# Layer 0's edge stage in a four-layer graph kernel: another order of the turn, lists in finer steps, and list work moved between two stages

## The chip, the cores and the metric

The kernel runs on one core of a Trainium2 chip. The metric is device time in microseconds (us), the median of three runs; lower is better. The core has a matrix engine (PE, with PEld for its weight loads), a vector engine (DVE), an activation engine (ACT), a general engine (POOL, here mostly for gathers by index) and a queue for transfers (SP). They run side by side and wait for one another through semaphores.

## The reference

Four graph layers follow one another on N = 4096 nodes with C = 256 channels and an adjacency matrix `adj` of N x N. Each is followed by a residual sum and a layer norm. The change concerns layer 0, which has 8 heads of 32 channels and 6 curvature features a node:

```python
h = (x @ W.T).reshape(n, H, D)
e_l = jnp.einsum('nhd,hd->nh', h, a_l)
e_r = jnp.einsum('nhd,hd->nh', h, a_r)
logits = jax.nn.leaky_relu(e_l[:, None, :] + e_r[None, :, :], negative_slope=0.2)
curv_pair = jnp.abs(curv_feats[:, None, :] - curv_feats[None, :, :])
logits = logits + gate * jnp.einsum('ijf,hf->ijh', curv_pair, Wc)
logits = jnp.where((adj > 0)[:, :, None], logits, jnp.float32(-1000000000.0))
attn = jax.nn.softmax(logits, axis=1)
out = jnp.einsum('ijh,jhd->ihd', attn, h).reshape(n, H * D)
...
x = _layernorm(x + out, axis=-1)
```

The adjacency is sparse, about 0.4% on average, and its first rows and columns are much denser than the rest: an edge (i, j) has the probability 0.0039 w_i w_j, where w falls as the inverse root of the node's number and has mean 1.

## The kernel before

**Stages of layer 0.** A prologue projects x and writes a table of node rows (264 values with the factor of the softmax, 8 head scores, 6 features) to memory. Then `rows0` works out the first chunk of 128 rows densely, in 32 tiles of columns, on times 187 to 436 us of the profile. After it `rows_by_edges`, the edge stage, works out the other 31 chunks by their edges, from about 440 to 1690 us. Meanwhile two background lanes prepare what comes later:

- Lane one, `list_edges`, makes the edge list of each chunk. `Lists.edges` turns adjacency rows into bf16; `Lists.steps` (L935) finds the columns of each row's edges (`max_index`, L943, 424 of them in all), sorts them (L949 to 960), counts them and writes `what` (node numbers by rank, and running starts), `half` and `from_middle`. Two small products on PE belong to it: `flags` (L923), 32 of one column each, which tell which tiles hold edges, and `last` (L973), running sums of the edge counts. After each fourth chunk `places` (L983) numbers the nodes that hold edges in pairs of chunks.
- Lane two, `list_pairs`, makes for the later layers, by `list_pair` (L1011), a list of the nodes that each pair of chunks needs: `rhs` (L1018 to 1022), four `here` (L1034), 32 products on PE (L1028) and a few steps on DVE. Each entry becomes a job `listed_mask`: a gather `pair_m` on POOL (L1055), and six jobs later a convert `pair_mb` on DVE (L1059) and a write by SP (L1060).

`lane` gives both lanes a step now and then. Its rates are steps per call: (3.0, 0.7) in `rows0`, one call a tile, and (1.4, 0.3) in the edge stage, one call for each tile of edges. Each call also does a pair job and a dense-mask job. `ends` (end steps of finished chunks, with layer 1's projection of them) takes a step a call as well.

**A turn of the edge stage.** A chunk's edges are cut into tiles of 128; blocks have 5 to 10 tiles, 64 blocks with 445 tiles in all. A block goes through these steps, in this logical order:

- `middle` (L615): ACT writes u, the distance of an edge number from the middle of each row's edges.
- `spread` (L621): DVE compares u with `half` (`of_row`, 1 where an edge belongs to a row, L624), and PE multiplies it by `what` (x, L627, two matmuls a tile), which gives each edge its row's list and values.
- `nodes` (L629): ACT copies the row's values (side, L632); DVE picks from x the column node of each edge (k L634, hit L636 and L638, node L640, idx L642).
- `gather` (L644): POOL issues one indirect gather a tile from the table into g, of which there are three buffers.
- `differences` (L650): DVE d (L654), PE transposes it (d_p, L656), ACT takes the positive part (dT, L658). `pair_terms` (L660): PE two products (e_p), ACT exponential (e, L666).
- `weights` (L668): DVE w, two steps. `values` (L675): DVE scales g by w (L678).
- `rows` (L680): ACT builds to_row, one activation a tile (L685) and one relu (L686). `add` (L688): PE sums g by row, two matmuls a tile (L691).

**What sets the order.** For PE, DVE and ACT the program order is written out (`manual_schedule`): what stands in the code first runs first on each of them. POOL and SP take their work in an order that the framework chooses. In turn i (L712 to 746) the code does spread(i+3), lane, differences(i+1), values(i), gather(i+2), pair_terms(i+1), lane, nodes(i+3), lane, add(i), rows(i+1), weights(i+1), middle(i+4), lane; the first three lane parts have n // 4 calls each, the last has the rest.

Of the kernel before, what the change touches and what calls it, by code (L numbers as in the profile page):

```python
# [49 lines left out]
F32 = mybir.dt.float32  # L50
# [6 lines left out]
ALU = mybir.AluOpType  # L57
AX = mybir.AxisListType
PSUM = bass.MemoryType.PSUM
DRAM = bass.MemoryType.DRAM  # L60

P = 128
IC = 512
# [15 lines left out]
def gnn_stack(ctx: ExitStack, tc: tile.TileContext, a: dict, out: bass.AP):  # L79
    nc = tc.nc  # L80
# [512 lines left out]
    def rows_by_edges(prepared, pair_w, neg_bound, ends, ps, lane):  # L593
# [8 lines left out]
        with ExitStack() as st:  # L602
# [8 lines left out]
            class Block:  # L611
# [3 lines left out]
                def middle(self):  # L615
# [2 lines left out]
                    self.u = two.tile([P, BT, P], F32, name="u", bufs=1)  # L618
                    nc.scalar.activation(self.u[:, 0:self.n], number[:, 0:self.n], AF.Abs, bias=self.lists.from_middle[:, self.b:self.b + 1])

                def spread(self):  # L621
                    n, ls = self.n, self.lists
                    of_row = two.tile([P, BT, P], F32, name="of_row")
                    nc.vector.tensor_scalar(of_row[:, 0:n], self.u[:, 0:n], ls.half, None, ALU.is_lt)  # L624
                    self.x = ps_x.tile([P, n, ls.K + SIDE], F32, name="x")
                    for t in range(n):
                        nc.tensor.matmul(self.x[:, t], of_row[:, t], ls.what, start=True, stop=True)  # L627

                def nodes(self):  # L629
                    n, K = self.n, self.lists.K  # L630
# [76 lines left out]
            def at(i, *what):  # L707
                if 0 <= i < B:
                    for w in what:
                        getattr(plan[i], w)()  # L710

            with tc.manual_schedule(engines={mybir.EngineType.PE, mybir.EngineType.DVE, mybir.EngineType.Activation}):  # L712
                for i in range(3):
                    at(i, "middle", "spread", "nodes")
                    if i < 2:
                        at(i, "gather")
                at(3, "middle")
                at(0, "differences", "pair_terms", "rows", "weights")
                late = []
                for i, blk in enumerate(plan):  # L720
                    c, n = blk.c, blk.n
                    share = n // 4
                    ends.put.extend(late)
                    late = []
                    at(i + 3, "spread")
                    lane(share)
                    at(i + 1, "differences")
                    blk.values()
                    at(i + 2, "gather")
                    at(i + 1, "pair_terms")  # L730
                    lane(share)
                    at(i + 3, "nodes")
                    lane(share)
                    if blk.t0 == 0:
                        ends.until(c - 2)
                        accs[c] = ps_acc.tile([P, VW], F32, name="acc")
                    last = blk.t0 + n == EDGE_TILES[c]
                    blk.add(accs[c], last)
                    if last:
                        acc = accs.pop(c)  # L740
                        late.append((lambda acc=acc: acc.rearrange("p (h d) -> p h d", h=H0), c))
                    at(i + 1, "rows", "weights")
                    at(i + 4, "middle")
                    lane(n - 3 * share)
                ends.put.extend(late)
                ends.until(NC)
                drain(ends.steps)

    def layer0(proj):
        lin = 1.0 - 0.2  # L750
        with ExitStack() as st:
# [119 lines left out]
            lists = st.enter_context(tc.tile_pool(name="l0_list", bufs=2))  # L871
            pool = st.enter_context(tc.tile_pool(name="l0_ps", bufs=1, space=PSUM))
            ps = tags(pool, ["pa", "pb"])
            lists_ps = st.enter_context(tc.tile_pool(name="l0_list_ps", bufs=1, space=PSUM))

            jobs, dense_jobs = [], []

# [6 lines left out]
            class Lists:  # L884
# [37 lines left out]

                def flags(self):  # L923

                    pf = ps([P, NT], "flags")
                    for T in range(NT):
                        nc.tensor.matmul(pf[:, T:T + 1], self.columns(T), ones_b[:, 0:1], start=True, stop=True)
                    return pf
# [6 lines left out]
                def steps(self, f):  # L935
                    c, K, kind = self.c, self.K, EDGE_PARTS[self.c]
                    S = sum(kind)
                    near = self.near
                    cand = lists.tile([P, S, 8], U16, name="cand")
                    cost = 0  # L940
                    for s, (at, W) in enumerate(self.spots):

                        nc.vector.max_index(cand[:, s], ones8, near[:, at:at + W])  # L943
                        cost += W + 100
                        if cost > 900:
                            cost = 0
                            yield
                    val = lists.tile([P, S, 8], F32, name="val", bufs=1)
                    nc.vector.tensor_tensor(val, widths[kind].unsqueeze(2).to_broadcast([P, S, 8]), cand, ALU.is_gt)  # L949
                    node = lists.tile([P, S, 8], F32, name="val_n", bufs=1)  # L950
                    nc.vector.tensor_tensor(node, firsts[kind].unsqueeze(2).to_broadcast([P, S, 8]), cand, ALU.subtract)
                    flags = self.flags()
                    nc.vector.tensor_mul(val, val, node)

                    top = lists.tile([P, KMAX], F32, name="top")
                    flat = val.rearrange("p s e -> p (s e)")
                    for k in range(0, K, 8):
                        nc.vector.max(top[:, k:k + 8], flat)
                        if k + 8 < K:
                            nc.vector.match_replace(flat, top[:, k:k + 8], flat, 0.0)  # L960
                            if k == 8:

                                nc.vector.tensor_scalar(f[:, c % BL, :], flags, 0.0, None, ALU.is_gt)
                                nc.vector.tensor_reduce(there[:, c:c + 1], flags, AX.X, ALU.add)
                            if k > 0:
                                yield
                    n_c = listed[:, c:c + 1]
                    hit = lists.tile([P, KMAX], F32, name="top_on")
                    nc.vector.tensor_scalar(hit[:, 0:K], top[:, 0:K], 0.0, None, ALU.is_gt, ALU.add, accum_out=n_c)
                    n_b = lists.tile([P, 1], BF16, name="n_b")  # L970
                    nc.vector.tensor_copy(n_b, n_c)
                    last = ps([P, 1], "last")
                    nc.tensor.matmul(last, upto, n_b, start=True, stop=True)  # L973
                    nc.vector.tensor_scalar(self.what[:, 0:K], top[:, 0:K], -1.0, float(N), ALU.mult, ALU.add)
                    nc.vector.tensor_scalar_mul(self.half, n_c, 0.5)
                    nc.vector.tensor_sub(self.what[:, K:K + 1], last, n_c)
                    mid = lists.tile([P, 1], F32, name="mid")
                    nc.vector.scalar_tensor_tensor(mid, last, -1.0, self.half, ALU.mult, ALU.add)
                    for b, (t0, _) in enumerate(blocks_of(c)):
                        nc.vector.tensor_scalar_add(self.from_middle[:, b:b + 1], mid, t0 * P + 0.5)  # L980
                    yield

            def places(k, f):  # L983
# [5 lines left out]
                yield  # L989
                W = BP * NT  # L990
                flat = g.rearrange("p b t -> p (b t)")
                upto_p = ps([P, W], "upto_p")
                nc.tensor.matmul(upto_p, upto, flat, start=True, stop=True)
                total_p = ps([P, W], "total_p")
                nc.tensor.matmul(total_p, ones_b, flat, start=True, stop=True)
                x = lists.tile([P, W], F32, name="place")
                nc.vector.tensor_tensor_scan(x, go_on.rearrange("p b t -> p (b t)"), total_p, 0.0, ALU.mult, ALU.add)
                nc.vector.tensor_copy(sizes[:, k * BP:(k + 1) * BP], x.rearrange("p (b t) -> p b t", t=NT)[:, :, NT - 1])
# [12 lines left out]
            def list_pair(q):  # L1011
# [9 lines left out]
                nc.vector.tensor_tensor(rhs[:, :, 0, :], rhs[:, :, 1, :], tiles.unsqueeze(2).to_broadcast([P, NT, A]), ALU.mult)  # L1021
                nc.vector.tensor_scalar_mul(rhs[:, :, 1, :], rhs[:, :, 1, :], row)
                yield
                pl = lists_ps.tile([P, 2, A], F32, name="list_p")

                def products(k, here):
                    for T in range(k * Q, (k + 1) * Q):
# [3 lines left out]
                for k in range(4):  # L1031
                    T = slice(k * Q, (k + 1) * Q)
                    here = lists.tile([P, Q, P], BF16, name="here", bufs=4)
                    nc.vector.tensor_tensor(here, count.unsqueeze(1).to_broadcast([P, Q, P]),  # L1034
                                            at[:, 1, b, T].unsqueeze(2).to_broadcast([P, Q, P]), ALU.is_equal)
                    due.append((k, here))
                    yield
                    if len(due) > 1:
                        products(*due.pop(0))
                products(*due.pop(0))  # L1040
                yield
                x = lists.tile([P, 2, A], F32, name="list")
                nc.vector.tensor_copy(x, pl)
# [132 lines left out]
                    ls.whole = True  # L1176
                return ls

            rows0(FIRST, ends, ps, lambda n: lane(n, (3.0, 0.7)), 2)

            def lane_e(n):
                for _ in range(n):
                    lane(1, (1.4, 0.3))
                    ends.step()

            rows_by_edges(prepared, pair_w, neg_bound, ends, ps, lane_e)
# [503 lines left out]
```

## Time and profile before

| what | value |
|---|---|
| runs | 3717.66, 3719.96, 3713.12 us; median 3717.66 |
| the profiled execution's own time | 4065.58 us |
| its span, first to last instruction | 4063.8 us |
| mean granted clock of PE | 0.78 |
| `rows0` | 187 to 436 us |
| edge stage, first to last `values` | 463.3 to 1673.8 us |
| gathers of g (L647) | 445, 482.2 us on POOL, 1084 ns each |
| pair gathers (L1055) | 251, 282.9 us on POOL, 1127 ns each |
| finds (L943) | 424, 192.9 us on DVE, 471 ns each |

The profiled execution is 348 us longer than the median, so a stage's length in it is not its length in a timed run. In the views, L12 is line 12 of the kernel; `out<-in` are the program's names; a wait reads "engine, what waited <- what released it: total us, times, longest". Lines of the timeline read "start, length, engine, line, operation, out<-in shapes, how many", with the idle time before and its releaser in square brackets. "issue" is time in which an engine waited for nothing that the profile shows; "remote" names a release that it doesn't trace to an instruction.

### The profile page before, as it was taken

Reading aid. Unit: us, or ns where it says so; the run is one execution under the profiler, and the core shown is the slowest. Engines: PE = TensorE matmul, PEld = TensorE weight load, DVE = VectorE, ACT = ScalarE, POOL = GpSimd, SP = SyncE. Lnnn points to the kernel's source line nnn. Section 1 sums busy time; section 2 is a strip of 40 time slices with the busy share of each in tenths; the row PEclk is TensorE's granted clock in tenths of the full one; section 3 lists DMA queues with packets and bytes.
Section 4 is the critical chain, followed back from the end, with each engine's and each line's share of the span. In section 5 each row is a group of like instructions: output and inputs, shape, how many; then the busy total and the mean of one; then the engine's idle time right before and its main releaser. Section 6 shows DMA issues by size and latency. Waiting matters only on the chain. (4 is left out here: it accounts for less than half of the span.)

```text
span 4063.8 us, 53164 instructions
## 1 busy us (share of the span) xinstructions
PE 2855.1 (70%) x15878; PEld 2107.2 (52%) x15878; DVE 2372.0 (58%) x7423; ACT 1320.8 (33%) x3748; POOL 1928.4 (47%) x1874
## 2 busy tenths in 40 slices
PE   7566544454666757677768887877688978987886
PEld 5355433343454545466653333333467757775664
DVE  5277677676555544345447888787444544544555
ACT  3344333343333334334443222223312231222233
POOL 0000465544676766234425755543166626643663
PEclk7577655666676666688878888989799989988998
DMA  4344577554334333244433333332334434434443
GB/s 140 94 139 138 162 236 235 178 151 148 106 107 111 108 107 97 85 148 125 123 95 114 99 97 97 94 91 70 116 106 115 110 116 113 120 83 138 137 140 90
DMA packets 348334, 495.62 MB, mean 122 GB/s; under 512 B 120828, under 2 KB 256866, under 8 KB 348034
## 3 DMA queue, kind: packets, MB, share of 16 engines
q0 software_dynamic: 87600, 252.16, 22.2%
q1 hardware_dynamic: 242008, 223.19, 18.7%
q10 hardware_dynamic: 18432, 16.79, 1.2%
q8 instruction: 131, 2.15, 0.2%
q14 instruction: 163, 1.34, 0.1%
HBM read 426.20 MB, written 65.72 MB: 121 GB/s over the span
## 5 line engine op out<-in xcount | busy, mean ns | idle before, releaser
L1271 POOL DMA_INDIRECT g<-table,pair_idx x1010 | 1106.7, 1096 | 814.2 <-issue 162.8
L647 POOL DMA_INDIRECT g<-table,idx x445 | 482.2, 1084 | 346.1 <-PE acc L691 183.1
L1560 PE MATMUL acc<-g,w 128*128 128x257 f32 x2448 | 599.7, 394 | 53.7 <-DVE w L1554 28.5
L1560 PEld LDWEIGHTS acc<-g,w 128*128 128x128 f32 x2448 | 470.3, 196 | 145.7 <-DVE w L1554 41.2
L1055 POOL DMA_INDIRECT pair_m<-in_adjT,cell x251 | 282.9, 1127 | 527.2 <-DVE mb L386 269.5
L1461 DVE SCALAR_TENSOR_TENSOR w<-R,g,mask 128x256 f32<-128x256 f32 x1004 | 425.1, 494 | 26.7 <-PE den L1474 19.5
L1554 DVE SCALAR_TENSOR_TENSOR w<-R,g,mask 128x256 f32<-128x256 f32 x612 | 281.4, 481 | 194.8 <-PE acc L1560 132.3
L1470 PE MATMUL num<-w,g 128*64 128x256 f32 x2008 | 326.5, 431 | 58.8 <-DVE w L1461 40.4
L203 PE MATMUL ph<-wx,xT 128*128 128x258 f32 (+3 forms) x640 | 255.8, 538 | 151.6 <-ACT xT L199 113.7
L691 PE MATMUL acc<-g,to_row 128*128 128x264 f32 x890 | 345.5, 567 | 10.6 <-issue 5.6
L1560 PE MATMUL acc<-V,w 128*128 128x257 f32 x1152 | 296.4, 398 | 32.8 <-DMA R<-r_d 11.5
L691 PEld LDWEIGHTS acc<-g,to_row 128*128 128x128 f32 x890 | 253.8, 294 | 81.5 <-issue 8.5
L627 PE MATMUL x<-what,of_row 128*128 128x40 f32 (+4 forms) x890 | 165.4, 361 | 165.8 <-DVE of_row L624 86.5
L1470 PEld LDWEIGHTS num<-w,g 128*64 128x64 f32 x2008 | 160.5, 151 | 207.6 <-DVE w L1461 110.3
L627 PEld LDWEIGHTS x<-what,of_row 128*128 128x128 f32 x890 | 158.1, 273 | 205.8 <-DVE of_row L624 92.7
L1560 PEld LDWEIGHTS acc<-V,w 128*128 128x128 f32 x1152 | 226.2, 200 | 74.4 <-ACT V L1540 18.1
L203 PEld LDWEIGHTS ph<-wx,xT 128*128 128x128 f32 x640 | 150.8, 257 | 214.3 <-ACT xT L199 145.1
L1570 ACT ACTIVATE y<-acc,inverse 128x256 f32<-128x256 f32 x96 | 45.5, 474 | 543.3 <-PE acc L1560 204.7
L1554 DVE SCALAR_TENSOR_TENSOR w<-R,V,mask 128x256 f32<-128x256 f32 x288 | 136.0, 480 | 121.3 <-PE acc L1560 56.5
L658 ACT ACTIVATE dT<-d_p 36x128 f32<-36x128 f32 (+5 forms) x64 | 17.2, 269 | 562.7 <-PE d_p L656 326.6
L943 DVE FIND_INDEX8 cand<-ones,near 128x8 uint16<-128x520 bf16 (+8 forms) x424 | 192.9, 471 | 0.0
L199 ACT ACTIVATE xT<-xT_p 128x128 f32<-128x128 f32 x384 | 102.7, 274 | 202.0 <-remote 107.1
(324 smaller groups left out, 4732.2 us busy)
## 6 DMA issues: line engine op xcount, KB each, us to landing
ai<-in_adj SPq DMA_DIRECT2D x124, 512.0 KB
mask<-listed_d SPq DMA_DIRECT2D x228, 128.0 KB
at<-in_adjT SPq DMA_DIRECT2D x96, 256.0 KB
mask<-mask_d SPq DMA_DIRECT2D x128, 128.0 KB
g<-table,pair_idx POOLq DMA_INDIRECT x1010
R<-r_d SPq DMA_DIRECT2D x56, 256.0 KB
table<-V POOLq DMA_DIRECT2D x12, 1032.0 KB
s<-y ACTq DMA_DIRECT2D x96, 128.0 KB
```

Of the source, the lines that this page charges most:

```text
L199: nc.scalar.activation(xT[:, kt, :], pt[:, kt, :], AF.Copy, accum_out=self.xs[:, kt, T:T + 1])
L203: nc.tensor.matmul(ph, xT[:, kt, :], self.wx[:, kt, :], start=kt == 0, stop=kt == 1 and self.bias is None)
L627: nc.tensor.matmul(self.x[:, t], of_row[:, t], ls.what, start=True, stop=True)
L647: nc.gpsimd.indirect_dma_start(self.g[:, t, :], None, table0[:, :], bass.IndirectOffsetOnAxis(ap=self.idx[:, t:t + 1], axis=0))
L691: nc.tensor.matmul(acc, self.to_row[:, t], self.g[:, t, 0:VW], start=self.t0 + t == 0, stop=last and t == n - 1)
L943: nc.vector.max_index(cand[:, s], ones8, near[:, at:at + W])
L1055: nc.gpsimd.indirect_dma_start(m[:, :], None, pair_cells, bass.IndirectOffsetOnAxis(ap=cell[:, k:k + 1], axis=0))
L1271: nc.gpsimd.indirect_dma_start(g[:, :], None, self.table[:, :], bass.IndirectOffsetOnAxis(ap=pair_idx[:, at:at + 1], axis=0))
L1461: nc.vector.scalar_tensor_tensor(w[:, h], R[:, h].rearrange("p t i -> p (t i)"), g[:, VW2 + h:VW2 + h + 1], m, ALU.max, ALU.mult)
L1470: nc.tensor.matmul(num[h % 2 * D2:(h % 2 + 1) * D2, h // 2, :], g[:, h * (D2 + 1):h * (D2 + 1) + D2], w[:, h], start=False, stop=last and ...
L1554: nc.vector.scalar_tensor_tensor(w, R[:, q * PW:(q + 1) * PW], g[:, C + 1:C + 2], m, ALU.max, ALU.mult)
L1560: nc.tensor.matmul(t, w[:, it * P:(it + 1) * P], g[:, 0:C + 1], start=k == 0, stop=last)
```

## The change

Four things change.

1. The order of the turn. `choose` (the of_row comparison) is taken out of `spread` and done one turn ahead. Turn i now does spread(i+3), values(i), add(i), lane, differences(i+1), choose(i+4), middle(i+5), lane, pair_terms(i+1), rows(i+1), nodes(i+3), gather(i+3), lane, weights(i+1), lane. So the gather is three blocks ahead in place of two (g keeps its three buffers), `middle` five ahead in place of four, `rows` comes ahead of `nodes`, and `add` comes right after `values`.
2. Lists in finer steps. The flags products are issued at the start of a list. There is a yield, an end of a lane step, between DVE's operands and the product that reads them (`last`), and between products and their readers (`last`, `places`). The 32 list products come in one go after the last `here` and a yield, instead of eight a step.
3. Rates: (1.5, 0.4) in `rows0` in place of (3.0, 0.7), and (1.5, 0.35) in the edge stage in place of (1.4, 0.3). By the order of the two programs' instructions, rows0 then holds 48 finds and 2 lists instead of 117 and 7, and the turns of the edge stage 296 finds and 26 lists, in turns 0 to 32, instead of 227 and 21, in turns 0 to 24; of the 60 `here` 56 instead of 52 fall into the edge stage, of the 15 rhs 14 instead of 12.
4. Memory: one fixed PSUM tile, `misc`, takes flags, `last`, places and list products, each at columns of its own, in place of the two rotating tiles that they shared with the turn's d_p and e_p (and of a tile of their own for list products).

```diff
+                def choose(self):
+                    n = self.n
+                    self.of_row = two.tile([P, BT, P], F32, name="of_row")
+                    nc.vector.tensor_scalar(self.of_row[:, 0:n], self.u[:, 0:n], self.lists.half, None, ALU.is_lt)
+
                 def spread(self):
                     n, ls = self.n, self.lists
-                    of_row = two.tile([P, BT, P], F32, name="of_row")
-                    nc.vector.tensor_scalar(of_row[:, 0:n], self.u[:, 0:n], ls.half, None, ALU.is_lt)
                     self.x = ps_x.tile([P, n, ls.K + SIDE], F32, name="x")
                     for t in range(n):
-                        nc.tensor.matmul(self.x[:, t], of_row[:, t], ls.what, start=True, stop=True)
+                        nc.tensor.matmul(self.x[:, t], self.of_row[:, t], ls.what, start=True, stop=True)
...
                 for i in range(3):
-                    at(i, "middle", "spread", "nodes")
-                    if i < 2:
-                        at(i, "gather")
-                at(3, "middle")
+                    at(i, "middle", "choose", "spread", "nodes", "gather")
+                at(3, "middle", "choose")
+                at(4, "middle")
                 at(0, "differences", "pair_terms", "rows", "weights")
...
+                    at(i + 3, "spread")
                     ends.put.extend(late)
                     late = []
-                    at(i + 3, "spread")
-                    lane(share)
-                    at(i + 1, "differences")
-                    blk.values()
-                    at(i + 2, "gather")
-                    at(i + 1, "pair_terms")
-                    lane(share)
-                    at(i + 3, "nodes")
-                    lane(share)
                     if blk.t0 == 0:
                         ends.until(c - 2)
                         accs[c] = ps_acc.tile([P, VW], F32, name="acc")
                     last = blk.t0 + n == EDGE_TILES[c]
+                    blk.values()
                     blk.add(accs[c], last)
                     if last:
                         acc = accs.pop(c)
                         late.append((lambda acc=acc: acc.rearrange("p (h d) -> p h d", h=H0), c))
-                    at(i + 1, "rows", "weights")
-                    at(i + 4, "middle")
+                    lane(share)
+                    at(i + 1, "differences")
+                    at(i + 4, "choose")
+                    at(i + 5, "middle")
+                    lane(share)
+                    at(i + 1, "pair_terms", "rows")
+                    at(i + 3, "nodes", "gather")
+                    lane(share)
+                    at(i + 1, "weights")
                     lane(n - 3 * share)
...
-            lists_ps = st.enter_context(tc.tile_pool(name="l0_list_ps", bufs=1, space=PSUM))
+
+            misc = st.enter_context(tc.tile_pool(name="l0_misc", bufs=1, space=PSUM)).tile([P, IC], F32, name="misc")
...
-                    pf = ps([P, NT], "flags")
+                    pf = misc[:, 0:NT]
...
                     cand = lists.tile([P, S, 8], U16, name="cand")
+                    flags = self.flags()
...
-                    flags = self.flags()
...
-                    last = ps([P, 1], "last")
-                    nc.tensor.matmul(last, upto, n_b, start=True, stop=True)
                     nc.vector.tensor_scalar(self.what[:, 0:K], top[:, 0:K], -1.0, float(N), ALU.mult, ALU.add)
                     nc.vector.tensor_scalar_mul(self.half, n_c, 0.5)
+                    yield
+                    last = misc[:, NT:NT + 1]
+                    nc.tensor.matmul(last, upto, n_b, start=True, stop=True)
+                    yield
...
-                upto_p = ps([P, W], "upto_p")
+                upto_p = misc[:, P:P + W]
                 nc.tensor.matmul(upto_p, upto, flat, start=True, stop=True)
-                total_p = ps([P, W], "total_p")
+                total_p = misc[:, 2 * P:2 * P + W]
                 nc.tensor.matmul(total_p, ones_b, flat, start=True, stop=True)
+                yield
...
-                pl = lists_ps.tile([P, 2, A], F32, name="list_p")
+                pl = misc[:, 3 * P:3 * P + 2 * A].rearrange("p (k a) -> p k a", k=2)
...
-                    if len(due) > 1:
-                        products(*due.pop(0))
-                products(*due.pop(0))
+                for some in due:
+                    products(*some)
...
-            rows0(FIRST, ends, ps, lambda n: lane(n, (3.0, 0.7)), 2)
+            rows0(FIRST, ends, ps, lambda n: lane(n, (1.5, 0.4)), 2)
...
-                    lane(1, (1.4, 0.3))
+                    lane(1, (1.5, 0.35))
```

## The prediction

> **What bounds the kernel now.** I read the page's head first, then the busy time by stretches, the waits of the edge stage, and last one turn of it in the timeline.
>
> ```profile
> span 4063.8 us, 53164 instructions
> PE 2855.1 (70%) x15878; PEld 2107.2 (52%) x15878; DVE 2372.0 (58%) x7423; ACT 1320.8 (33%) x3748; POOL 1928.4 (47%) x1874
> ```
>
> No engine is full over the span, and the chain of waits is followed only through the last row of layer 3, which says nothing of layer 0. So the stage itself has to be read. The starts of the 64 `values` products (L678) mark the turns: turn 0 at 463.3 us, turn 26 at 1081.2, turn 52 at 1480.5, turn 63 at 1673.8. Lists are made in the first of these three parts, pair masks are read in the first two. The busy-time table over rows0, then over the three parts (busy time and instructions of PE, PEld, DVE, ACT, POOL, then PE clock, DMA share, GB/s):
>
> ```profile
> 187.00:436.00 249.00, 156.59 (x1398) 137.22 (x1397) 181.75 (x806) 110.63 (x181) 20.96 (x22) 0.73 0.43 133
> 463.30:1081.20 617.90, 294.39 (x1788) 238.28 (x1787) 436.94 (x1559) 211.07 (x484) 339.00 (x312) 0.60 0.60 179
> 1081.20:1480.50 399.30, 268.62 (x1101) 202.75 (x1101) 201.64 (x527) 148.11 (x430) 277.14 (x249) 0.64 0.39 108
> 1480.50:1673.80 193.30, 138.26 (x493) 102.12 (x493) 83.67 (x202) 78.53 (x226) 114.52 (x102) 0.67 0.35 97
> ```
>
> That is 23.8, 15.4 and 17.6 us a turn, 1210 us in all, and in none of the parts is an engine busy for more than 71%. Engines wait for one another. The waits between 440 and 1690 us (total, times, longest):
>
> ```profile
> ACT dT L658 <- PE d_p L656: 326.6, 33, 20.8
> POOL g L647 <- PE acc L691: 183.1, 30, 18.3
> ...
> ACT dT L658 <- remote: 88.4, 7, 18.6
> PE x L627 <- DVE of_row L624: 86.5, 25, 14.8
> DVE k L634 <- ACT side L632: 80.9, 22, 18.6
> PE last L973 <- DVE n_b L971: 70.4, 7, 16.6
> DVE d L654 <- DMA g<-table,idx: 65.7, 18, 9.7
> DVE f L963 <- remote: 46.5, 8, 13.3
> ```
>
> ACT has nothing to do before dT, POOL cannot gather until `add` frees a buffer, PE waits for the row choice. These are ends of one ring: of_row, spread, d_p, dT, e_p, e, side, k to idx, w, of_row again. One 6-tile turn gives its step times:
>
> ```profile
> 1308.14 1.80 DVE L678 TENSOR_TENSOR g<-g,w 128x1584 f32<-128x1584 f32 x1
> 1308.28 0.40 PE L656 MATMUL d_p<-ident,d 128*36 128x128 f32 x1 [7.15 <-DVE d L654]
> 1308.71 0.27 ACT L658 ACTIVATE dT<-d_p 36x128 f32<-36x128 f32 x1 [12.26 <-issue]
> 1309.03 0.66 PE L663 MATMUL e_p<-pair_w,dT 36*128 36x48 f32 x2 [0.36 <-issue]
> ...
> 1310.20 4.62 PE L691 MATMUL acc<-g,to_row 128*128 128x264 f32 x12
> 1310.31 0.21 ACT L666 ACTIVATE e<-e_p 128x48 f32<-128x48 f32 x1 [1.33 <-PE e_p L664]
> 1310.42 0.23 ACT L632 COPY side<-x 128x90 f32<-128x90 f32 x1
> 1310.53 1.86 ACT L685 ACTIVATE to_row<-count,side 128x128 f32<-128x128 f32 x6
> 1312.43 0.84 ACT L686 ACTIVATE to_row<-to_row 128x768 f32<-128x768 f32 x1
> 1312.62 0.14 DVE L634 TENSOR_TENSOR k<-place,x 128x6 f32<-128x6 f32 x1
> ```
>
> What matters here: `add` (4.6 us on PE) and `to_row` (2.7 us on ACT) run at the same time, and side comes ahead of to_row. Neither is in the ring.
>
> **What the skill says.** "TensorE: Matmul & The Clock Gate", Architectural detail: matmuls start and complete in program order. So what stands behind `add` on PE waits for `add`; the trace agrees, in the turn above d_p, e_p and `add` start one after the other (1308.28, 1309.03, 1309.62, 1310.20). "PSUM — Partial Sum Buffer", section on bank collisions: engines must not touch one bank together, and a guard is wanted. The trace agrees: x is read by ACT (side) and DVE (k), and after a stall k starts 0.03 us after side ends (side 1016.45 for 0.25, k at 1016.73). So k follows side wherever side goes. The first page again, on the clock gate: an idle PE falls to a slower clock. Here the clock is 0.60 to 0.67 in the stage; an 18-matmul `add` at 1587.44 took 7.27 us, a 13-matmul one at 1559.81 took 3.06.
>
> **The change part by part.** Costs at nothing: the shared PSUM tile; flags issued at a list's start (same matmuls, and it removes "f <- remote", 46.5 us); `choose` a turn ahead (same DVE instruction, 0.70 us; it removes the PE wait for of_row); three more yields a list (no instruction). All 32 list products in one go are the same matmuls, about 0.05 us each.
>
> *The turn.* In the new order PE has add(i), then d_p(i+1), e_p(i+1), lists, spread(i+4); ACT has dT, u(i+5), e, to_row(i+1), relu, side(i+3); DVE has values, lane 1, d, choose, lane 2, k(i+3) to idx, lane 3, w(i+1), lane 4, values(i+1). Hence a ring with both `add` and `to_row` in it: values, add, d_p, dT, e_p, e, to_row and relu, side, k to idx, w, next values. For six tiles: 1.80 + 0.26 (hand-over) + 4.45 (add's start to the next PE step) + 0.43 + 0.32 + 1.28 + 0.21 + 2.75 + 0.25 + 1.36 + 0.44 = 13.55 us. The parts that grow with tiles (1.80, 4.45, 2.75) make 1.5 us a tile, so 4.55 + 1.5n: 14.45, 14.25 and 17.75 us for the mean n of 6.6, 6.5 and 8.8 in the three parts. DVE's lanes 1 and 2 (some 4.3 us with d, choose) lie beside add to to_row and cost nothing as long as they stay under those 9 us; lanes 3 and 4 are in the ring: by the new order of instructions and the old mean durations 7.1, 3.4 and 0.5 us a turn. PE's lane work between add and e_p adds 0.75, 0.85 and 1.05. Turns: 22.3, 18.5, 19.3 us; 26 x 22.3 + 26 x 18.5 + 11 x 19.3 = 1273 us. For stalls inside that ring I add 25: 9.0 for the seven ACT table loads at e (1283 ns each) and 16 for waits on DMA of masks and pairs in lanes 3 and 4, of which the old trace has 48 us in all places (17.0 + 18.0 + 13.2). Edge stage 1298 against 1210: +88.
>
> *Gathers.* Ordered a turn earlier, three g buffers as before. POOL needs 1.25 us an issue (0.95 busy, 0.30 between): (7 + 3.6 pair reads) x 1.25 = 13.2 us a turn, under the ring. The 65.7 us that DVE waited for g go; so does "g <- acc", without worth of its own, since the ring is later. All DMAs stay the same in number, and nothing is moved on SP but mask writes with their converts. New: gather(i+3) waits for idx, and pair reads behind it on POOL wait too; they are read 6 jobs later (some 20 us), so nothing until that is gone.
>
> *Rates in rows0.* 3.0 to 1.5 and 0.7 to 0.4: by instruction order 69 finds (about 0.5 us with load), 5 lists (about 5 us of sorting), 4 `here` (1.2), 2 rhs (2.1) leave: 34.5 + 25 + 4.8 + 4.2 = 69 us of DVE, and that stage's list tiles take 14 to 18 us with 10 to 12 of DVE list work, others 2.6 to 6. DVE is the busiest there (182 of 249), so I take -70. Bounds: -40 (its 66.8 us of waits for ACT's e L494 grow) to -95 (waits go with it). The same work comes back in lanes of the edge stage; it is in the 7.1 above.
>
> *Sum against the profiled execution* (4065.6 us, span 4063.8): +88 - 70 = +18. But the median is 3717.7, 348 us less, and the trace cannot tell where the 348 lie. If they are spread over every duration, 18 x 0.914 = +16. If they are idle times such as the "remote" ones (88.4 + 46.5 + 25.9 = 161 us in the stage), the old loop was 1210 - 348 x 1210/4064 = 1106 in a timed run, while my new one, put together from durations and not from idle time, stays: 1298 - 1106 - 70 = +122. Between them, +70: 3790 us.
>
> **Rivals.**
> *Faster: the freed waits count.* `add` first gives the g buffer back some 10 us earlier, spread no longer waits for of_row (86.5), list ends no longer hold PE (70.4 + 46.5). Then a turn is set by load: DVE busy 16.8 us in part one, POOL 13.2 after it: 26 x 16.8 + 37 x 13.2 = 925 against 1210. A third of those 285 and the 70 of rows0, by 0.914, give -151: 3567. For it: the large waits. Against: they are ends of a ring, and the new ring is longer. It decides if turns of part two stay under 14 us.
> *Hidden.* rows0's gain and part one's (618 to 580) are given back by the later turns: +16, or about 3725, down to 3705. For it: the plain sum above.
> *Slower still, a cold PE.* `add` is now in the ring and comes after 10 us of PE idling; at 0.44 us a matmul instead of 0.37 it costs 0.95 us a turn, +60, on the upper end of the sum: 3717.7 + 122 + 60 = 3900.
> *POOL blocked.* Pair reads held behind gather(i+3) make converts in lanes 3 and 4 wait: 5 us a turn over 52 turns, +260 at worst, half of it likelier: 3920. It decides when a convert finds its pair read later than 6 jobs.
>
> **How the numbers follow.** What a measurement here can tell from no change is about 0.2%, 7.4 us. My forecast (ring, 3735 to 3870): 0.50. Hidden, 3705 to 3735: 0.12, of which 0.05 within 0.2%, 0.05 slower, 0.02 faster. Cold PE: 0.12. POOL: 0.06. Faster: 0.20, mostly 3560 to 3700. So slower 0.73, same 0.05, faster 0.22. The range 3640 to 3900 leaves out about 0.1 at each end; the likeliest case's own is 3735 to 3870.
>
> **What would show it.** Right: `k` waiting for ACT's side after to_row in most turns; d_p starting at add's end; turns near 22, 18 and 19 us; rows0 near 180 us; no wait of `d` for the gather; PE no more waiting for of_row. Wrong: part two under 15 us a turn, or POOL issuing without idle time (then load bounds), or converts waiting on pair_m, or rows0 still above 230 us.

## The result, and the profile after

The changed kernel takes 3862.59 us (median of four runs, 3859.93 to 3870.40) against 3717.56 us before (3713.12 to 3719.96): 1.0395 times before, 95% interval 1.0377 to 1.0413, or +145 us. The forecast was 3790 us, +72 us: the sign was right and the result lies in the stated range, but the change is twice the forecast.

Whole groups of runs were of one of two kinds, in which before took 3713 to 3726 us or 4031 to 4104 us, and the first profile of before (4065.6 us) is of the longer kind, the timed runs and the first profile after (3870.4 us) of the shorter. This section therefore compares two profiles of the shorter kind, taken together: `pair_before` (3725.58 us) and `pair_after` (3868.08 us), 142.5 us apart.

The page's first line of each, before and after:

```profile
span 3723.9 us, 53164 instructions
```

```profile
span 3866.3 us, 53147 instructions
```

The busy time by stretches, for the three parts of the edge stage (turns 0 to 25, 26 to 51, 52 to 62; columns as in the prediction). Before:

```profile
457.30:1018.40 561.10, 297.04 (x1788) 240.46 (x1787) 436.76 (x1560) 211.14 (x484) 344.87 (x312) 0.61 0.65 197
1018.40:1389.30 370.90, 267.62 (x1100) 202.20 (x1100) 202.59 (x528) 148.08 (x429) 280.12 (x249) 0.65 0.42 116
1389.30:1572.90 183.60, 134.91 (x493) 100.39 (x493) 83.37 (x202) 78.67 (x227) 117.58 (x102) 0.70 0.37 102
```

After:

```profile
383.60:1001.90 618.30, 287.13 (x1712) 234.84 (x1711) 421.48 (x1525) 207.46 (x484) 342.55 (x308) 0.60 0.59 175
1001.90:1498.60 496.70, 270.10 (x1348) 208.12 (x1347) 277.11 (x876) 171.90 (x466) 304.32 (x273) 0.62 0.42 120
1498.60:1720.30 221.70, 136.08 (x499) 101.51 (x497) 81.01 (x195) 72.80 (x219) 113.64 (x95) 0.65 0.30 81
```

The reader sees three things. The stage starts 74 us earlier (383.6 against 457.3), which is list work gone from rows0. The 63 turns take 1336.7 us in place of 1115.6, +221. And little of this is more work: over all the turns DVE is busy for 780 us in place of 723, with the lists brought in, and PE for 693 in place of 700; the last part has nearly the same instructions, less busy time on DVE, ACT and POOL and 1 us more on PE, and takes 38 us more. From the start of the last `values` to the end it is 2151 us before and 2146 after. So -74 + 221 - 5 = +142: the whole difference is in layer 0, and the loss is in the edge stage.

The waits of the edge stage, before (440 to 1570 us):

```profile
ACT dT L658 <- PE d_p L656: 501.8, 56, 20.8
PE x L627 <- DVE of_row L624: 158.3, 40, 12.0
...
POOL g L647 <- PE acc L691: 99.6, 29, 13.1
...
DVE k L634 <- ACT side L632: 80.2, 26, 13.2
DVE d L654 <- DMA g<-table,idx: 71.3, 21, 12.2
```

After (382 to 1716 us):

```profile
ACT dT L661 <- PE d_p L659: 638.4, 48, 22.4
DVE k L637 <- ACT side L635: 416.5, 59, 26.2
POOL g L650 <- issue: 397.2, 416, 20.4
...
PE acc L694 <- issue: 221.3, 36, 16.9
```

The waits that the change was to remove are almost gone (PE for of_row is 10 us in the whole profile, d for the gather 1 us), and one has grown fivefold: DVE's k waits for side 59 times in 64 turns, 416 us. (POOL's 397 us before g are off the path that follows, since d waits only 1 us for g.)

The timeline of one turn after, with six tiles like the turn shown in the prediction (from the first profile after):

```profile
1309.29 1.80 DVE L681 TENSOR_TENSOR g<-g,w 128x1584 f32<-128x1584 f32 x1
1311.19 5.47 PE L694 MATMUL acc<-g,to_row 128*128 128x264 f32 x12 [5.65 <-issue]
...
1315.35 0.18 DVE L295 BATCH_NORM_AGGREGATE mv<-bn_st 128x2 f32<-128x6 f32 x1
1316.50 0.27 PE L659 MATMUL d_p<-ident,d 128*36 128x128 f32 x1
1316.81 0.27 ACT L661 ACTIVATE dT<-d_p 36x128 f32<-36x128 f32 x1 [9.75 <-PE d_p L659]
...
1318.04 1.85 ACT L688 ACTIVATE to_row<-count,side 128x128 f32<-128x128 f32 x6
1319.92 0.84 ACT L689 ACTIVATE to_row<-to_row 128x768 f32<-128x768 f32 x1
1320.67 0.22 ACT L635 COPY side<-x 128x90 f32<-128x90 f32 x1
1320.92 0.16 DVE L637 TENSOR_TENSOR k<-place,x 128x6 f32<-128x6 f32 x1 [5.38 <-ACT side L635]
...
1323.61 0.20 DVE L674 TENSOR_TENSOR w<-side,g 128x48 f32<-128x48 f32 x1
...
1325.88 1.80 DVE L681 TENSOR_TENSOR g<-g,w 128x1584 f32<-128x1584 f32 x1
```

This is one chain across three engines: values, add, d_p, dT, e_p, e, to_row, relu, side, k to idx, w, values again, 16.6 us. (Left out of the lines are e_p and e, the steps from k to idx, and DVE's lane work behind idx and behind w.) The wait of add is put down to "issue", but add starts 0.1 us after values ends. DVE has no more lane work after 1315.5 and idles 5.4 us until k. In the old order `add` and `to_row` ran side by side and outside of this path. The Trainium skill ("PSUM — Partial Sum Buffer", "PSUM bank collisions raise a hardware error") states that two engines must not access one bank of PSUM at the same time and that software has to guard it. In this trace the two readers of x, side on ACT and k on DVE, come one after the other: side ends at 1320.89 and k starts at 1320.92.

### The profile page after: what moved, and what is told of

Its sections match the earlier page's. It is cut to its first block, busy times and chain, and to the rows that moved or that the text cites. A ratio compares the mean times of both kernels' runs of the same rounds, so it can differ in the third digit from the quotient of the medians.

```text
span 3868.7 us, 53147 instructions
## 1 busy us (share of the span) xinstructions
PE 2727.9 (71%) x15878; PEld 2043.7 (53%) x15878; DVE 2369.0 (61%) x7423; ACT 1317.3 (34%) x3748; POOL 1962.7 (51%) x1874
## 5 line engine op out<-in xcount | busy, mean ns | idle before, releaser
L1276 POOL DMA_INDIRECT g<-table,pair_idx x1010 | 1121.0, 1110 | 600.2 <-issue 95.0
L650 POOL DMA_INDIRECT g<-table,idx x445 | 522.1, 1173 | 444.8 <-issue 398.3
L1565 PE MATMUL acc<-g,w 128*128 128x257 f32 x2448 | 578.0, 384 | 35.5 <-DVE w L1559 35.4
L1565 PEld LDWEIGHTS acc<-g,w 128*128 128x128 f32 x2448 | 461.9, 191 | 112.0 <-DVE w L1559 47.8
L1060 POOL DMA_INDIRECT pair_m<-in_adjT,cell x251 | 261.9, 1043 | 453.5 <-DVE mb L386 315.2
L203 PE MATMUL ph<-wx,xT 128*128 128x258 f32 (+3 forms) x640 | 241.7, 514 | 86.2 <-ACT xT L199 86.1
L637 DVE TENSOR_TENSOR k<-place,x 128x6 f32<-128x6 f32 (+5 forms) x64 | 10.4, 163 | 428.1 <-ACT side L635 428.1
L630 PEld LDWEIGHTS x<-what,of_row 128*128 128x128 f32 x890 | 168.6, 290 | 99.0 <-issue 91.0
L197 PE MATMUL xT_p<-ident,y 128*128 128x128 f32 x320 | 77.7, 331 | 154.3 <-ACT y L331 147.8
L630 PE MATMUL x<-what,of_row 128*128 128x40 f32 (+4 forms) x890 | 177.0, 379 | 10.2 <-DVE of_row L624 10.2
```

Source lines behind the costliest of these rows:

```text
L197: nc.tensor.transpose(pt[:, kt, :], x[:, kt * P:(kt + 1) * P], ident)
L203: nc.tensor.matmul(ph, xT[:, kt, :], self.wx[:, kt, :], start=kt == 0, stop=kt == 1 and self.bias is None)
L630: nc.tensor.matmul(self.x[:, t], self.of_row[:, t], ls.what, start=True, stop=True)
L650: nc.gpsimd.indirect_dma_start(self.g[:, t, :], None, table0[:, :], bass.IndirectOffsetOnAxis(ap=self.idx[:, t:t + 1], axis=0))
L1060: nc.gpsimd.indirect_dma_start(m[:, :], None, pair_cells, bass.IndirectOffsetOnAxis(ap=cell[:, k:k + 1], axis=0))
L1276: nc.gpsimd.indirect_dma_start(g[:, :], None, self.table[:, :], bass.IndirectOffsetOnAxis(ap=pair_idx[:, at:at + 1], axis=0))
```

## The experiments

Ratios are to the kernel before in the same group of runs, with the 95% interval; the last column has the median of before in that group. Microseconds can be compared only between groups in which before took about the same time. The ring theory is that of the prediction: add and to_row have come into the closed path of a turn. The list theory is its rival: the loss comes from the list work brought into the stage.

| run | what it is | ratio to before | interval | before, us |
|---|---|---|---|---|
| new_turn | before, only the new order of the turn | 1.0458 | 1.0421 to 1.0496 | 4078.14 |
| old_turn | after, the old order of the turn | 0.9876 | 0.9844 to 0.9907 | 4078.14 |
| side_first | after, rows behind nodes | 0.9992 | 0.9967 to 1.0018 | 4078.14 |
| add_late | after, add back near the turn's end | 0.9950 | 0.9928 to 0.9971 | 3719.28 |
| add_late_side_first | both | 0.9761 | 0.9745 to 0.9777 | 3719.28 |
| k_late | both, nodes and gather behind lane three | 0.9767 | 0.9743 to 0.9791 | 4084.66 |
| choose_early | old turn, row choice one ahead | 0.9824 | 0.9808 to 0.9841 | 3719.28 |
| before_rates | before, only the new rates | 0.9939 | 0.9914 to 0.9965 | 4084.66 |
| old_turn_old_rates | before, only finer lists and fixed PSUM tile | 1.0000 | 0.9980 to 1.0019 | 4084.66 |

**The turn against all the rest: new_turn and old_turn.** The edit is the turn's part of the change (choose, spread, the loop), put into before, or taken out of after.

> The kernel before with only the new order of the turn (and row choice one ahead, gather three ahead); lists, rates and PSUM tiles as before. Ring theory: the whole loss without the gain in rows0: 3860 to 3950 us. List theory: within 30 us of 3717.

> The changed kernel with the turn's order of before (row choice within spread, gather two ahead, add late); lists in finer steps, rates and the fixed PSUM tile stay changed. Ring theory: the turn is all of the loss, so this is at or below before by part of what rows0 gave (70 to 80 us): 3640 to 3720 us. List theory: it keeps most of the loss, 3800 to 3860.

Measured 1.0458 and 0.9876. The order of the turn alone costs 4.6%, more than the whole change; all the rest gains 1.2%. The list theory falls: it expected new_turn near 1.00 and old_turn above 1.02. (The ring theory's microseconds, over the 3717 us of the first runs, ask for 1.038 to 1.063 and 0.979 to 1.001.)

**Side ahead of to_row: side_first.**

```diff
-                    at(i + 1, "pair_terms", "rows")
+                    at(i + 1, "pair_terms")
                     at(i + 3, "nodes", "gather")
                     lane(share)
-                    at(i + 1, "weights")
+                    at(i + 1, "rows", "weights")
```

> The changed kernel with rows (to_row and relu on ACT) after nodes and beside weights, so that side no longer stands behind to_row. Ring theory: to_row and relu (2.75 us for six tiles, about 3.0 on average) leave the ring, 64 turns x 3 = -190 us at most; in the first 33 turns DVE's lanes fill part of it, so -100 to -190: 3670 to 3760 us, and the wait of k for side (428 us) falls below 250. List theory (the loss comes from list work brought into the stage, the turn's order doesn't matter): within 20 us of 3862.

Measured 0.9992, four per cent of before below after's 1.0395, with to_row moved behind side. Before took 4078 us in this group, so the microseconds of the expectation don't apply, but in ratio it asked for 0.987 to 1.011. The wait of k for side came to 269 us, a little above the 250 that were expected:

```profile
DVE k L637 <- ACT side L635: 269.1, 37, 22.9
```

**Add behind the relays: add_late, and both together: add_late_side_first.** In both, `blk.add` and the lines that keep its accumulator go from behind `values` to just ahead of weights; the second has the edit of side_first as well.

```diff
                     blk.values()
-                    blk.add(accs[c], last)
...
                     lane(share)
+                    blk.add(accs[c], last)
                     at(i + 1, "weights")
```

> The changed kernel with add moved from the front of the turn to just ahead of weights, so that d_p and e_p no longer stand behind it; rows stays ahead of nodes. Ring theory: add with its hand-over (4.7 us for six tiles, 5.2 on average) leaves the ring; lane 1, d, choose on DVE come into it instead where they were hidden (1 to 3 us), so -2 to -4 us a turn, -130 to -250 us against after_again, that is 0.97 to 1.01 of before. If add first does not matter: 1.03 to 1.05 of before.

> Both moves undone: add late and rows behind nodes; row choice still one ahead, gather three ahead, lists and rates changed. Ring theory: both parts of the ring are gone, so near or below old_turn (0.9876 of before): 0.96 to 1.00. If the two parts hide one another: no better than side_first (0.999).

Measured 0.9950 (3706.16 us) and 0.9761 (3631.22 us), both where the ring theory expected them. From first to last values the profiles have 1330 us in `after_again`, 1174 in add_late, 1101 in add_late_side_first: add is worth 156 us, to_row 73 more. Alone, to_row was worth about 4% or 150 us (side_first), so the two overlap. What binds the turns once one of them is out is not shown; DVE is busy for 421 of the 516 us of turns 0 to 25 in add_late_side_first, against 421 of 618 in pair_after. The waits of add_late, then of add_late_side_first:

```profile
ACT dT L661 <- PE d_p L659: 543.0, 51, 19.6
...
PE d_p L659 <- DVE d L657: 296.9, 48, 17.6
DVE k L637 <- ACT side L635: 244.9, 53, 18.9
```

```profile
ACT dT L661 <- PE d_p L659: 479.8, 51, 19.9
...
PE d_p L659 <- DVE d L657: 263.9, 48, 17.6
...
DVE k L637 <- ACT side L635: 115.6, 37, 12.3
```

k's wait falls from 416 to 245 to 116 us, and PE waits for DVE's d (264 us), where in the changed kernel d was done before d_p could start (1312.13 and 1316.50 in the turn above). This version is faster than both kernels, by 2.4% against before. It keeps the early row choice, the gather three ahead, the finer lists and the rates, and undoes only "sums first" and "rows ahead of nodes".

**The row choice alone: choose_early.** The old turn, with these lines:

```diff
                     blk.values()
+                    at(i + 4, "choose")
...
-                    at(i + 4, "middle")
+                    at(i + 5, "middle")
```

> The old turn of old_turn with one part of the new one: the row choice one block ahead, behind values, and middle five ahead. Ring theory: spread no longer waits for of_row (124 us in old_turn), and PE, DVE and POOL loads are next: 1 to 2 us a turn, so 0.955 to 0.980 of before. If of_row's wait was only the end of another wait: the 0.988 of old_turn.

Measured 0.9824, between the two expectations, with its interval ending just short of that of old_turn. PE's wait for of_row falls from 124 us in old_turn to 10, and the time falls by only half a per cent, some 20 us: most of that wait was the end of another. The profile also answers the list theory once more, in an execution of the same kind as the pair: with all the list work brought into the stage, but values late and add and to_row in their old places, the 63 turns take 1113.0 us, as in pair_before (1115.6), and not the 1336.7 of pair_after.

**Rates and finer lists apart: before_rates, old_turn_old_rates.** The first changes only the four rates in before, the second has the lists' part of the diff only.

> The kernel before with only the new rates, (1.5, 0.4) and (1.5, 0.35). Old_turn (rates, finer lists and fixed PSUM tile together, old turn) took 0.988 of before. If the rates are what gave that (rows0 is 77 us shorter and the edge stage takes over the list work for about 25 us): 0.983 to 0.992. If the finer steps gave it: 0.995 to 1.01.

> The kernel before with only the finer lists and the fixed PSUM tile, old turn and old rates. If finer steps take DVE's and PE's waits on last, places and list products out of the turn (last <- n_b 70 us, f <- 47 us in the first profile): 0.985 to 0.995. If these waits were ends of the ring: 0.997 to 1.003. If two or three more steps a list delay the lists without use: above 1.003.

Measured 0.9939, between the two expectations, and 1.0000, where waits that are ends of the ring were to put it. The finer lists and the fixed PSUM tile alone do nothing measurable, the rates alone give 0.6%, half of what all of these give together (0.9876). In its profile before_rates starts the edge stage at 392 us in place of 461, but its turns take 1283 us in place of 1194 to 1220; with the finer steps (old_turn) they take 1235. A reading that fits is that the rates move work out of rows0 and the finer steps keep it from holding up the turns that receive it; it rests on one profile each and is not shown.

**Lanes ahead of k: k_late.**

```diff
-                    at(i + 3, "nodes", "gather")
                     lane(share)
+                    at(i + 3, "nodes", "gather")
```

> The fastest so far (add late, rows behind nodes: 0.976 of before) with nodes and gather behind the third lane part, so that DVE has list work to do while side is on its way. There k still waited 123 us for side. Ring theory: half or more of this goes, -40 to -110 us: 0.947 to 0.966 of before. If DVE and POOL loads bound that version already: 0.972 to 0.980; worse if the later gather makes d wait (34 us there).

Measured 0.9767, no different from 0.9761. The ring theory missed here: it expected at least half of k's wait for side to go, and 103 us of it were left. The number lies where the loads of DVE and POOL as the bound would put it, but no engine is full in add_late_side_first (DVE 82% in turns 0 to 25, POOL 71% in turns 26 to 51, PE 74% after them), so what bounds that version stays open.

**The same programs again.** `before_again`, `before_third`, `before_fourth`, `after_again` and the pair are unedited.

> The kernel before, profiled a second time. If the 348 us by which its first profile exceeded the timed runs were idle time, durations of single instructions stay (values 2065 ns, find 471 ns) and the waits shrink: span near 3716 us, first to last values near 1100 us in place of 1210, the time after the last values near 2150 us as in the changed kernel's profile (3868.7 - 1719.6) in place of 2390. If the excess was spread over durations, these are 8 to 9% shorter.

> The kernel before, profiled where it takes about 3718 us, if these runs fall there. The changed kernel's two profiles there left 2145 us after the last values and began the edge stage at 382 us. If the excess of the first profile over the timed runs was waits that such a run doesn't have: no wait of 'remote' and little of 'issue', durations of values (2065 ns) and to_row (395 ns) within 2% of the first profile, first values near 459 us, first to last values 1113 us (3718 - 1 - 2145 - 459). If it was spread over durations, 8 to 9% off each of them.

> The kernel before, profiled where it takes about 3718 us, if this run falls there; expectation as for before_third: first values near 459 us, first to last values 1113 us, no 'remote' waits, durations within 2% of the first profile. Where it takes about 4075 us again, nothing new.

> The changed kernel once more, profiled beside the kernel before, because the kernel before took 4078 us in the last runs where it took 3718 in the first ones, and its first profile (4066 us) is of the slower kind. If the slower kind takes the same share from every kernel, this is 1.0395 times before (near 4239 us where before is 4078) with an end of the edge stage near 1770 to 1830 us; new_turn ended it at 1860 and side_first at 1693.

The three of before took 4073.82, 4072.93 and 4031.34 us, with 1214, 1220 and 1194 us from first to last values, much as in the first profile. `after_again` took 3862.38 us, with 1330 us, in a group in which before took 3719 us, so what was expected of it beside 4078 us was not tested. The pair settles what the first profile's excess is:

> The kernel before, profiled in one go with pair_after, so that both loops can be laid side by side on one chip. Where before takes about 3718 us: first to last values 1113 us, no 'remote' waits. Where it takes about 4070 us: 1210 us as in its other profiles.

> The changed kernel beside pair_before. Where before takes about 3718 us: first to last values 1330 us, as in its other two profiles, 217 more than pair_before. Where before takes about 4070 us: new_turn (old lists and rates) had 1402 there; with the ring of the same steps I expect 1400 to 1440, about 200 more than pair_before, and 4210 to 4260 us in all.

They took 3725.58 and 3868.08 us, with 1115.6 and 1336.7 us from first to last values, 221 apart, where 1113, 1330 and 217 were expected. Two groups of the edge stage, from the first profile of before and from pair_before:

```profile
L685 ACT ACTIVATE to_row<-count,side 128x128 f32<-128x128 f32 x445 | 136.8, 395 | 0.0
L678 DVE TENSOR_TENSOR g<-g,w 128x1584 f32<-128x1584 f32 (+5 forms) x64 | 132.2, 2065 | 0.0
```

```profile
L685 ACT ACTIVATE to_row<-count,side 128x128 f32<-128x128 f32 x445 | 136.8, 395 | 0.0
L678 DVE TENSOR_TENSOR g<-g,w 128x1584 f32<-128x1584 f32 (+5 forms) x64 | 132.0, 2063 | 0.0
```

These durations are equal to a tenth of a per cent, and PE's busy time between first and last values is 701 us in the first profile and 700 in pair_before. The "remote" waits of the first profile's stage (88.4, 46.5 and 25.9 us) have no counterpart in pair_before, which has no "remote" wait at all. So in the edge stage the excess of 95 us is waiting, and not slower work.

## Why the prediction was half right

**The ring: right.** The path that the prediction wrote down from the order of instructions is the one in the timeline after, step by step, and the experiments agree: with add and to_row taken out of it the loss is gone. Mean times from start to start, worked out from the trace of pair_after:

| step | forecast, six tiles | turns 0 to 25, mean 6.6 tiles | turns 26 to 51, mean 6.5 tiles |
|---|---|---|---|
| values to add | 2.06 | 2.52 | 2.84 |
| add to d_p | 4.45 and PE's lanes 0.75, 0.85 | 5.58 | 5.70 |
| d_p to dT to e_p to e to to_row | 2.24 | 2.25 | 2.34 |
| to_row to side | 2.75 | 2.92 | 2.84 |
| side to k | 0.25 | 0.28 | 0.25 |
| k to w | 1.36 and lane 3 | 3.73 | 2.30 |
| w to values | 0.44 and lane 4 | 6.50 | 2.83 |
| a turn | 22.3 and 18.5 | 23.8 | 19.1 |

The signs that it named appeared: k waits for side in most turns, d_p starts where add ends, the waits for the gather and for of_row are almost gone.

**The ring's size: 39 us short.** 1337 us against 1298. The three parts are 39, 16 and 9 us longer than their turns in the forecast, 64 in all, and the 25 us set aside for stalls cover part of that. The largest term at fault is the DVE part of the first turns: k to values is 10.2 us, where 7.1 of lanes and 1.8 of own steps made 8.9. Half a microsecond of it is k to idx: 1.36 us was read from a later turn with lists of 24, while those of the first chunks are up to 64 long, and in turns 0 to 25 it takes 1.89. The other term is a wait that the ring of the forecast does not have. In most turns add starts 0.1 us after values ends, but in turns 16, 27, 35, 36, 52, 57 and 61 it starts 5.5 to 11.6 us after: layer 1's projection of a finished chunk and spread stand before it on PE, and in the new order d_p of the next turn stands behind it. So in turns 26 to 51 values to add is 2.84 us where values and hand-over make 2.2, which is the 16 us of that part; in the first eight turns of the last part (20.2 us a turn for 19.3) it is 5.0 us for 2.9.

**rows0: right.** -70 forecast; from its first step e (L510) to its last rows0 takes 173 us in pair_after and 243 in pair_before, and the edge stage starts 74 us earlier.

**Gathers: right.** d waits 1 us for g, POOL is busy for at most 61% of a part, and converts wait 4 us for pair reads, less than before (18).

**The step that failed: "Sum against the profiled execution".** The mechanism was right; the term that was mis-sized is "Between them, +70". The profile of before was 348 us longer than the timed runs, and the prediction took the middle of two readings of that: excess spread over every duration (+16), or excess in idle times (+122). The runs showed the second: in the edge stage the durations are the same and the waits differ. The old loop is 1115.6 us in an execution of the timed kind, where the second reading had worked out 1106. The middle took 52 us off it. From that reading everything adds up: +122, +39 for the ring, -10 for the old loop, -4 for rows0, -5 for what follows the last values, is +142, the difference of the pair. That the forecast still had the right sign and range rests on the ring, not on the middle.

The trace of before alone held a hint that was given too little weight. A sum of durations can be compared only with a time that has no untraced waits in it, and the prediction itself counted 161 us of "remote" waits in the stage. Nothing in the trace spoke for durations that were 9% too long, so the upper reading, 3840 us, was the better supported.

**Two readings of lines.** The 13-matmul add "at 1559.81" is the rest of a sum that starts at 1558.43 and takes 4.43 us; the view began in its middle. And PE is busy for 71.5% of the third part, just over the 71% named. No term of the sum rests on either.

**The rivals.** "Faster: the freed waits count" falls: these waits were freed, and turns of the second part take 19.1 us, not under 14. "Hidden" falls, since the later turns gave back more than rows0's gain. "A cold PE" was not it: add to d_p is 5.6 to 5.7 us, where the forecast's terms make 5.6 for 6.6 tiles. "POOL blocked" did not appear: converts wait 4 us for pair reads in the whole stage.

## What to carry to other kernels

Where the program order of several engines is written by hand and no engine is full, look for the longest closed path of a turn through the engines, and write it down for the new order before anything moves. Here two long steps that the next relays don't need (add, to_row) did harm ahead of the short relays (d_p, dT, e_p, e, side) on their engines, and with both behind them again the ratio went from 1.0395 to 0.9761. A wait that disappears is no gain until the path that takes its place is shorter; here nearly all of 158 us of PE's and 71 us of DVE's waits went, and the stage became 221 us longer. When a profile and the timed runs disagree, find out whether durations or waits differ before a number built from durations is subtracted from a length read off the profile.

## What was not expected of the hardware

The same program, with the same instructions, took 3713 to 3726 us in some groups of runs and 4031 to 4104 us in others, nearly a tenth apart. The granted clock is 0.81 in the profile of the shorter kind and 0.78 to 0.80 in the four of the longer. The longer kind has "remote" waits in every profile (429 to 515 us in the four of before, over all engines), the shorter has none in any kernel's. The busy time of DVE and ACT over the whole profile is the same within 0.2%. PE's is 92 us longer in the first profile of before than in pair_before (2855.1 against 2762.6), nearly all of it after the edge stage; so there the excess (2390 us in place of 2151 from the last values to the end) is not all waiting.

What tells the two kinds apart was not found. Where the chip is on record, two chips gave only the shorter kind and three only the longer, but each was used at one time only, so the chip and its condition at that time can't be told apart. The loss by the order of the turn shows in both: new_turn lost 4.6% where before took 4078 us, and the whole change lost 4.0% where it took 3718.
